# Seven-product V for the second pair of groups, moved from slots 11 to 17 into slots 72 to 84

## The chip, the cores and the metric

The kernel runs on one core of one Trainium2 chip. The metric is the time of one execution on the device, in microseconds (us); less is better. All data are fp32.

## The reference

One post-norm layer over a batch of two sequences of 512 tokens, width 512: grouped-query attention with 32 heads in 8 groups of 4, head size 128, and then a feed-forward block with four active low-rank experts. Cut to what matters here:

```python
q = hidden_states @ Wq + bq;  k = hidden_states @ Wk + bk;  v = hidden_states @ Wv + bv
q = _rope(q, pos);  k = _rope(k, pos)
scores = jnp.einsum('bgrsd,bgtd->bgrst', qg, k) / jnp.sqrt(D)
scores = jnp.where(causal, scores, finfo.min)
probs = softmax(scores)
ctx = jnp.einsum('bgrst,bgtd->bgrsd', probs, v)
x = layernorm(x + (ctx @ Wo + bo))
x = layernorm(x + ffn(x))
```

The change is about `v` (the projection of the hidden states by `Wv`) for one pair of groups and one batch, and about the addition of `bo`.

## The kernel before

**Units and slots.** A unit is one group of one batch: 16 units, in the order group 0 batch 0, group 0 batch 1, group 1 batch 0 and so on until the last two groups. The order of all work is written out by hand in slots. Slot T computes one block of scores (`score(T)`: 128 rows, which are 32 query positions of four heads), so a unit takes 16 slots (`UNIT`), and the widths within a unit go 32, 64, ... 512 columns because of the causal mask: score T has 32 x (T mod 16 + 1) columns, so that a slot can be found in the trace by the width. Four slots make a part p (a tile of 128 query positions). `slot(T)` emits, in this order: steps of the Q products, steps of the K or V products, the output products, score T, then `weigh` (context from weighted V, 12 slots after the part's first score); then the copies, maxima, exponentials and additions that belong to earlier slots; and last whatever was hung onto the slot with `put`. Each engine takes its instructions in the order in which they were emitted.

**What a score goes through.** TensorE writes score T to one of two PSUM buffers of tile `sc`. VectorE takes the masked maximum (L570), ScalarE the exponential (L577), and only then is the buffer free for score T + 2. VectorE inverts the sum (L581), ScalarE multiplies (L585), VectorE transposes in blocks of 32 (L593, L595). After a part's four slots the blocks are sent by SyncE's queue to memory (`db`, L603) and read back in the transposed arrangement (`pT`, L611), and `weigh` (L618) multiplies them with V.

**Products by seven.** Two neighbouring heads of Q, two groups of K or V, and two parts of the output projection are computed together as a 2 by 2 block product with seven instead of eight half products; the sums and differences of input blocks are formed first (`x_sums`, `w_sums`, `kv_sums`, `ctx_sums` on GpSimd, `wo_sums` on VectorE). Results are combined by copies on ScalarE (`q_copy`, `kv_out`) and additions on VectorE (`q_sum`, L490; `kv_out`, L546). A Q product that starts a new sum in the bank `qy` must wait until VectorE has added the bank's old content (L490).

**V.** V is made for pairs of groups: pair p is groups 2p and 2p + 1. Pair 0 is made plainly for both batches, by `v_tile`: for a tile of 128 tokens four products of 128 by 128 with 256 columns, in the PSUM tile `wx`, which the output products use only from slot 21 on, and then `v_out`, one copy on ScalarE (L357). Pairs 1 to 3 go by `kv_at`: in frames of 16 slots that begin at slot 8, 24, 40, ..., the four frames of a period hold K of batch 0, K of batch 1, V of batch 0 and V of batch 1 of the next pair, in seven steps (`KV_STEPS`: 0, 2, 4, 6, 8, 10 and 12 slots after the frame's start). The seven products of V need `kv_sums`, four operations on GpSimd, and end in four copies on ScalarE (L544) and three additions on VectorE (L546). One V is the exception: pair 1 of batch 0 (groups 2 and 3), which is made plainly in slots 11, 13, 15 and 17, so that the frame of slots 72 to 87 has no K or V products in it. Every V has its buffer out of three; V of pair 1 is first used by `weigh` in slot 76.

A plain tile and a step of seven, in the code's words (`product` for V is written out in `kv_products`):

```python
nc.tensor.matmul(psq["v", gg, t], lhsT=xT[:, c, ts(t, P)], rhs=wvs[gg][:, c, :], ...)      # x4 (c), 256 columns
nc.tensor.matmul(ps[:, ts(t, P)], lhsT=xt[:, c, ts(t, P)], rhs=w[:, c, :], ...)           # x2 (t) x2 (c), 128 columns
```

In the trace each fp32 product appears as two matmuls, each with its own weight load.

**Around slots 11 to 24.** These are the first slots with everything under way. VectorE also has here the rotations of Q and K (L378, L381, L385), the copies `lp_bc`, `arT`, `b_jar` and `bmT` of the feed-forward weights (slots 12 to 14; `arT` and `bmT` wait for small products `ta` and `tbm` that TensorE does in slots 13 and 14, after the slot's score and V tile), and the four sums of the first output weights (`wo_sums`, L647, slots 16 to 19). GpSimd has the second half of each rotation (L386), the weight sums of Q, the sums of contexts (L437 to L440), and eight additions of the output bias `bo` to the residual `x_sb`, one per token tile, in slots 12 to 19 (L906). The bias comes in a tile `bo_bc` of a pool that closes at slot 20, whose space goes to a pool (`late`) first written in slot 40 by `kv_sums`, on GpSimd too.

Of the kernel before, what the change touches and what calls it, by code (L numbers as in the profile page):

```python
# [12 lines left out]
ALU = mybir.AluOpType  # L13
# [4 lines left out]
G = 8  # L18
# [11 lines left out]
def postln_layer_kernel(  # L30
# [33 lines left out]
    nc = tc.nc  # L64
    B, S, HID = x.shape
    NT = B * S // P
    TPB = S // P
# [10 lines left out]
    UNIT = S // BLK  # L78
    VG = 2
# [30 lines left out]
    ps_wo = ctx.enter_context(tc.tile_pool(name="ps_wo", bufs=1, space=bass.MemoryType.PSUM))  # L110
# [3 lines left out]
    x_sb = const.tile([P, NT, HID], F32, name="x_sb")  # L114
# [34 lines left out]
    def load_k(g, queue=nc.sync):  # L149
        wk_g = wts.tile([P, KC, D], F32, tag="wk_g", name=f"wk_{g}")  # L150
        queue.dma_start(out=wk_g, in_=Wk[:, ts(g, D)].rearrange("(c p) n -> p c n", p=P))
        wqk["k", g] = wk_g
# [12 lines left out]
    def load_wv(gg):  # L165
        wv_g = wts.tile([P, KC, VN], F32, tag="wv_g", name=f"wv_{gg}", bufs=1)
        nc.sync.dma_start(out=wv_g, in_=Wv[:, ts(gg, VN)].rearrange("(c p) n -> p c n", p=P))
        wvs[gg] = wv_g
# [38 lines left out]
    bo_bc = setup.tile([P, HID], F32, name="bo_bc")  # L207
# [63 lines left out]
    def gather_experts(step):  # L271
        if step == 0:
            gather(ar_act[:EAR, :], lora_A.rearrange("e r n -> (e r) n"), idx["a"])
        elif step == 1:
            gather(ar_act[EAR : EAR + EA, :], router_W, idx["e"])
        else:
            a = step - 2
            gather(b_act[:, a, :], lora_B.rearrange("e (p j) r -> (e p) (j r)", j=BJ), idx["b"][:, a : a + 1])
# [65 lines left out]
    def v_mm(gg, t, c, pool, tag):  # L344

        if c == 0:
            psq["v", gg, t] = pool.tile([P, VN], F32, tag=tag, name="pv")
        nc.tensor.matmul(  # L348
            psq["v", gg, t], lhsT=xT[:, c, ts(t, P)], rhs=wvs[gg][:, c, :], start=(c == 0), stop=(c == KC - 1))

    def v_of(gg, b):
        if (gg, b) not in v_sb:
            v_sb[gg, b] = work.tile([P, TPB, VN], F32, tag="v", name=f"v_{gg}_{b}", bufs=3)
        return v_sb[gg, b]

    def v_out(gg, t):
        nc.scalar.copy(v_of(gg, t // TPB)[:, t % TPB, :], psq["v", gg, t])  # L357
# [77 lines left out]
    def strassen_sums(engine, a11, a12, a21, a22, s1, s2, s4):  # L435

        engine.tensor_tensor(s1, a21, a22, ALU.add)  # L437
        engine.tensor_tensor(s2, s1, a11, ALU.subtract)
        engine.tensor_tensor(s4, a12, s2, ALU.subtract)
        engine.tensor_tensor(a21, a11, a21, ALU.subtract)  # L440
# [59 lines left out]
    def kv_block(kind, p, h, c):  # L500
        if kind == "k":
            return wqk["k", VG * p + h][:, CH * c : CH * (c + 1), :]
        return wvs[p][:, CH * c : CH * (c + 1), ts(h, D)]

    def kv_sums(kind, p):
        w = kvs[kind, p] = late["pool"].tile([P, 3, CH, D], F32, tag="kvs", name=f"kvs_{kind}_{p}")
        strassen_sums(
            nc.gpsimd, *(kv_block(kind, p, h, c) for h in range(2) for c in range(2)), *(w[:, m] for m in range(3)))
# [376 lines left out]
    def put(slot, f):  # L885
        extra.setdefault(slot, []).append(f)
# [3 lines left out]
    def v_tile(gg, t, pool, tag):  # L890
        for c in range(KC):
            v_mm(gg, t, c, pool, tag)

    for k in range(2 + EA):
        put((-5, -4, -3, 7, 8, 9)[k], lambda k=k: gather_experts(k))
    for n, gg, t in [(n, 0, TPB + 1 + k) for k, n in enumerate((-4, 4, 6))] + [(2 * t + 11, 1, t) for t in range(TPB)]:
        put(n, lambda gg=gg, t=t: v_tile(gg, t, ps_wo, "wx"))
        put(n + 1, lambda gg=gg, t=t: v_out(gg, t))
    for k in range(2):
        put((5, 12)[k], lambda k=k: prior_weights(k + 1))  # L900
        put(13 + k, lambda k=k: lora_weights(k))
# [1 line left out]
    put(6, lambda: load_wv(1))  # L903
    put(17, lambda: load_wo(1))
    for t in range(NT):
        put(12 + t, lambda t=t: nc.gpsimd.tensor_tensor(x_sb[:, t, :], x_sb[:, t, :], bo_bc, ALU.add))  # L906

    def q_from(u, k):

# [15 lines left out]
    for p in range(1, G // VG):  # L925
        at = PERIOD * p
        put(13 if p == 1 else at - PERIOD + 9, lambda p=p: load_k(VG * p))
        put(37 if p == 1 else at - PERIOD + 13, lambda p=p: load_k(VG * p + 1))
        put(40 if p == 1 else at - 2 * UNIT + 3, lambda p=p: kv_sums("k", p))
        if p > 1:  # L930
            put(at - PERIOD + 37, lambda p=p: load_wv(p))
        put(at + (UNIT if p == 1 else 0) + 3, lambda p=p: kv_sums("v", p))

    def kv_at(T):

        frame, o = divmod(T - KV_FROM, UNIT)
        p, k = divmod(frame + B, VG * B)
        kind, b = "kv"[k // B], k % B
        if 0 < p < G // VG and (kind, p, b) != ("v", 1, 0):
            return (kind, p, b), o  # L940
        return None, None

# [6 lines left out]
    for n in range(NSETS - 2):  # L949
        at = {0: (-5, -4, -3, -2), NSETS - 4: (-16, -15, -15, -13), NSETS - 3: (-11, -9, -6, -5)}.get(n, (0, 1, 1, 3))  # L950
# [18 lines left out]
    def slot(T):  # L969
# [10 lines left out]
        if 0 < uk < PLAIN_K and l < KC:  # L980
            k_mm(uk, l)
        kv, o = kv_at(T)
        if kv and o in KV_STEPS:
            kv_products(*kv, KV_STEPS[o])
# [335 lines left out]
```

## Time and profile before

| | |
|---|---|
| time, median of 3 runs | 817.26 us (816.86 to 817.88) |
| time of the profiled execution | 816.9 us |
| its span, first to last instruction | 815.1 us |
| TensorE matmuls busy | 807.0 us (99%) |
| TensorE weight loads busy | 609.7 us (75%) |
| VectorE busy | 609.8 us (75%) |
| ScalarE busy | 384.9 us (47%) |
| GpSimd busy | 338.6 us (42%) |
| mean granted TensorE clock | 0.998 |

Starts and durations are in microseconds from the span's start. The profile names the engines PE (TensorE matmuls), PEld (TensorE's weight loads, which overlap the matmuls), DVE (VectorE), ACT (ScalarE), POOL (GpSimd) and SP (SyncE, which issues most transfers). The end of a matmul is modelled and overlaps the next one's start, so the price of a matmul is read from the distance of starts, not from its duration. A row of the timeline is a run of equal instructions: start, length, engine, line, operation, output<-inputs, shape and count; in brackets, how long the engine was idle before it and what ended that.

### The profile page before, as it was taken

To read this page: it belongs to the slowest core of one execution; us is meant where nothing else is said; L and a number is where in the kernel's file an instruction comes from. 1 tells how busy PE (TensorE), PEld (TensorE's weight loads), DVE (VectorE), ACT (ScalarE), POOL (GpSimd) and SP (SyncE) were. 2 spreads that over 40 slices of the span, in tenths; PEclk is the share of its full clock that TensorE was granted. 3 is DMA by queue.
4 is the path that set the end of the run, shared out by engine and by line. 5 is a ranking of instruction groups with operands and counts; after the bars stand their busy time and mean duration, and the time that the engine had idled before them with its cause. 6 is when DMAs were issued, how large, how long until landed. Compare 5 with 4: busy or idle time off the path is not lost.

```text
span 815.1 us, 11389 instructions
## 1 busy us (share of the span) xinstructions
PE 807.0 (99%) x3457; PEld 609.7 (75%) x3457; DVE 609.8 (75%) x1978; ACT 384.9 (47%) x1074; POOL 338.6 (42%) x392
## 2 busy tenths in 40 slices
PE   9999999999999999999999999999999999999996
PEld 7887777777777778777777778777777878656575
DVE  4778877687879886787867876787888689973455
ACT  2355454444545454545435454544545454663244
POOL 8666645421444345322443245343464333420033
PEclk9999999999999999999999999999999999999999
DMA  9025736355455637264544637365453726674211
GB/s 298 26 72 143 219 83 202 91 130 156 134 169 136 182 93 219 77 181 129 147 147 121 178 82 219 91 160 179 137 146 91 232 66 181 189 263 143 77 39 65
DMA packets 84415, 116.00 MB, mean 142 GB/s; under 512 B 6525, under 2 KB 64237, under 8 KB 82306
## 3 DMA queue, kind: packets, MB, share of 16 engines
q1 hardware_dynamic: 83154, 114.71, 49.0%
q8 instruction: 27, 0.44, 0.2%
q10 hardware_dynamic: 752, 0.42, 0.2%
q14 instruction: 34, 0.28, 0.1%
q0 software_dynamic: 448, 0.14, 0.1%
HBM read 71.21 MB, written 44.04 MB: 141 GB/s over the span
## 4 chain that ended last, share of the span: by engine, by line
PE 96%; POOL 1%; DVE 1%; ACT 1%; issue 0%; POOLq 0%
PE pc L618 17%; PE sc L562 15%; PE qx L450 14%; PE wx L450 12%; PE qy L450 10%; PE wy L450 9%; PE kx L450 4%; PE vx L528 4%; PE po L694 3%; PE py L788 3%; PE pv L348 3%; PE pp L365 1%; PE tp L285 1%; PE py L829 1%; POOL zt L191 0%; POOL act_er L220 0%
## 5 line engine op out<-in xcount | busy, mean ns | idle before, releaser
L577 ACT ACTIVATE p<-sc,nmax 128x288 f32<-128x288 f32 (+15 forms) x256 | 124.2, 485 | 197.7 <-DVE nmax L570 175.2
L570 DVE CUSTOM_DVE_ANT_0 sc<-sc,maskw 128x288 f32<-128x288 f32 (+15 forms) x256 | 114.2, 446 | 136.3 <-PE sc L562 134.7
L618 PE MATMUL pc<-pT,v 128*128 128x512 f32 x320 | 165.3, 599 | 0.0
L562 PE MATMUL sc<-kT,qT 128*128 128x160 f32 (+15 forms) x512 | 161.7, 398 | 0.3 <-ACT p L577 0.3
L386 POOL TENSOR_TENSOR qT<-q,t 128x512 f32<-128x512 f32 x64 | 88.0, 1376 | 176.1 <-DVE q L385 165.0
L585 ACT ACTIVATE p<-p,den 128x288 f32<-128x288 f32 (+15 forms) x256 | 133.2, 521 | 0.0
L562 PEld LDWEIGHTS sc<-kT,qT 128*128 128x128 f32 x512 | 96.1, 190 | 21.9 <-issue 8.1
L625 ACT ACTIVATE ctxT<-pc,bqkT 128x512 f32<-128x512 f32 x64 | 44.0, 688 | 114.8 <-PE pc L618 114.7
L437 POOL TENSOR_TENSOR cs<-ctxT 128x256 f32<-128x256 f32 x28 | 22.4, 801 | 158.5 <-PE wy L450 95.4
L593 DVE STREAM_TRANSPOSE zt<-p 128x128 f32<-128x128 f32 (+2 forms) x192 | 81.7, 426 | 0.0
L486 ACT COPY q<-qx 128x256 f32<-128x256 f32 x128 | 47.4, 370 | 51.4 <-PE qx L450 49.8
L618 PEld LDWEIGHTS pc<-pT,v 128*128 128x128 f32 x320 | 57.1, 190 | 18.7 <-issue 5.7
L450 PE MATMUL qx<-xs,wq 128*128 128x256 f32 x256 | 66.3, 381 | 0.0
L450 PEld LDWEIGHTS qx<-xs,wq 128*128 128x128 f32 x256 | 47.3, 190 | 23.2 <-issue 18.4
L595 DVE STREAM_TRANSPOSE zt<-p 128x32 f32<-128x32 f32 (+3 forms) x256 | 57.6, 225 | 0.0
L450 PE MATMUL wx<-wo,ctxT 128*128 128x256 f32 x224 | 57.5, 379 | 0.0
L378 DVE SCALAR_TENSOR_TENSOR t<-q,bqkT,rope_sb 64x512 f32<-64x512 f32 x64 | 52.3, 818 | 3.5 <-ACT q L486 1.7
L381 DVE SCALAR_TENSOR_TENSOR t<-q,bqkT,rope_sb 64x512 f32<-64x512 f32 x64 | 50.3, 786 | 1.5
L577 ACT ACTIVATION_READ_ACCUMULATOR p<-sc,nmax 128x1 f32 x256 | 49.8, 194 | 0.0
L385 DVE SCALAR_TENSOR_TENSOR q<-q,bqkT,rope_sb 128x512 f32<-128x512 f32 x64 | 48.1, 751 | 0.1
L450 PEld LDWEIGHTS wx<-wo,ctxT 128*128 128x128 f32 x224 | 42.5, 190 | 7.0 <-issue 1.4
L680 DVE TENSOR_TENSOR x_sb<-wx,x_sb 128x256 f32<-128x256 f32 x112 | 47.0, 420 | 0.0
(234 smaller groups left out, 1468.3 us busy)
## 6 DMA issues: line engine op xcount, KB each, us to landing
db<-zt SPq DMA_DIRECT2D x64, 256.0 KB, 4.3
pT<-db SPq DMA_DIRECT2D x16, 1024.0 KB, 4.8
db<-zt SPq DMA_DIRECT2D x64, 192.0 KB, 3.3
pT<-db SPq DMA_DIRECT2D x16, 768.0 KB, 4.4
wq<-in_L_attn_Wq_dram SPq DMA_DIRECT2D x20, 512.0 KB, 5.1
wo<-in_L_attn_Wo_dram SPq DMA_DIRECT2D x10, 1024.0 KB, 9.0
db<-zt SPq DMA_DIRECT2D x64, 128.0 KB, 2.4
pT<-db SPq DMA_DIRECT2D x16, 512.0 KB, 4.2
```

The source lines that it names most:

```text
L378: nc.vector.scalar_tensor_tensor(t2[lo, :], q[hi, :], b_ap[hi, :], rope_sb[hi, 1, :], ALU.add, ALU.mult)
L381: nc.vector.scalar_tensor_tensor(t2[hi, :], q[lo, :], b_ap[lo, :], rope_sb[lo, 1, :], ALU.add, ALU.mult)
L385: nc.vector.scalar_tensor_tensor(t1, q, b_ap, rope_sb[:, 0, :], ALU.add, ALU.mult)
L386: nc.gpsimd.tensor_tensor(dst, t1[:, :].rearrange("p (n s) -> p n s", s=BLK), t2[:, :].rearrange("p (n s) -> p n s", s=BLK), ALU.add)
L450: nc.tensor.matmul(ps, lhsT=wt[:, c, :], rhs=xt[:, c, :], start=start and c == 0, stop=c == CH - 1, skip_group_check=True)
L562: nc.tensor.matmul(sc[s][:, :w], lhsT=qT[u][:, i * QB + n].rearrange("p r s -> p (r s)"), rhs=kT[u][:].rearrange("p n s -> p (n s)")[:, :w ...
L570: nc.vector.tensor_tensor_reduce(sc[s][:, :w], sc[s][:, :w], maskw[:, S - w :], -SCALE, -MASKED, ALU.add, ALU.min, nmax[s])
L577: nc.scalar.activation(ptile[s][:, :w], sc[s][:, :w], AF.Exp, bias=nmax[s], scale=-1.0, accum_out=rden[s])
L585: nc.scalar.activation(ptile[s][:, :w], ptile[s][:, :w], AF.Copy, scale=rden[s])
L593: nc.vector.transpose(z[:, :, last - i : last, n, :].rearrange("p q j s -> p j q s"), ptile[s][:, : i * P])
L595: nc.vector.transpose(z[:, : n + 1, last, n, :], ptile[s][:, i * P : w])
L618: nc.tensor.matmul(psc[p], lhsT=v_sb[g // VG, b][:, j, ts(g % VG, D)], rhs=pT[p][:, :, ts(j, P)], start=(j == 0), stop=(j == i))
```

## The change

V of pair 1, batch 0, is no longer made by `v_tile` and `v_out` in slots 11 to 18. The exception in `kv_at` goes, so it is made by seven products in slots 72, 74, 76, 78, 80, 82 and 84, like all later ones, with copies and additions in slots 73 to 85. The weight sums for it (`kv_sums("v", 1)`) move from slot 83 to slot 67, because batch 0 now needs them too. Of the eight additions of the output bias, which were in slots 12 to 19, one each, the eight now stand in slots 11, 13, 15, 17, 19, 23, 26 and 28.

```diff
-    for n, gg, t in [(n, 0, TPB + 1 + k) for k, n in enumerate((-4, 4, 6))] + [(2 * t + 11, 1, t) for t in range(TPB)]:
-        put(n, lambda gg=gg, t=t: v_tile(gg, t, ps_wo, "wx"))
-        put(n + 1, lambda gg=gg, t=t: v_out(gg, t))
+    for k, n in enumerate((-4, 4, 6)):
+        put(n, lambda t=TPB + 1 + k: v_tile(0, t, ps_wo, "wx"))
+        put(n + 1, lambda t=TPB + 1 + k: v_out(0, t))
...
-        put(12 + t, lambda t=t: nc.gpsimd.tensor_tensor(x_sb[:, t, :], x_sb[:, t, :], bo_bc, ALU.add))
+        put((11, 13, 15, 17, 19, 23, 26, 28)[t], lambda t=t: nc.gpsimd.tensor_tensor(x_sb[:, t, :], x_sb[:, t, :], bo_bc, ALU.add))
...
-        put(at + (UNIT if p == 1 else 0) + 3, lambda p=p: kv_sums("v", p))
+        put(at + 3, lambda p=p: kv_sums("v", p))
...
-        if 0 < p < G // VG and (kind, p, b) != ("v", 1, 0):
+        if 0 < p < G // VG:
```

## The prediction

> **What bounds the kernel now.** I read the page first, then the waits of TensorE, then the timelines of TensorE and VectorE around slots 11 to 24, then the same for the frames after slot 72.
>
> ```profile
> span 815.1 us, 11389 instructions
> PE 807.0 (99%) x3457; PEld 609.7 (75%) x3457; DVE 609.8 (75%) x1978; ACT 384.9 (47%) x1074; POOL 338.6 (42%) x392
> PE sc L562 <- ACT p L577: 0.3, 1, 0.3
> ```
>
> TensorE is full, and its longest wait on a score is 0.3 us. A matmul taken out is time gained, provided that nothing else becomes the limit at that place. So two things must be found: the price of the plain V and of the seven products, and how much room the other engines leave in slots 11 to 24. First the price, from distances of starts (timeline of TensorE):
>
> ```profile
> 62.75 0.81 PE L562 MATMUL sc<-kT,qT 128*128 128x384 f32 x2
> 63.40 1.89 PE L348 MATMUL pv<-wv,xT 128*128 128x256 f32 x8
> 65.13 0.86 PE L562 MATMUL sc<-kT,qT 128*128 128x416 f32 x2
> ...
> 282.51 1.05 PE L528 MATMUL vx<-wv,xT 128*128 128x128 f32 x8
> 283.40 0.76 PE L562 MATMUL sc<-kT,qT 128*128 128x352 f32 x2
> ```
>
> A plain tile costs 65.13 - 63.40 = 1.73 us, a step of seven 283.40 - 282.51 = 0.89 us. Then the room (waits of VectorE from 63.3 to 91.95 us, and its timeline):
>
> ```profile
> DVE arT L296 <- PE ta L294: 2.4, 1, 2.4
> DVE sc L570 <- PE sc L562: 0.8, 1, 0.8
> DVE bmT L303 <- PE tbm L302: 0.6, 1, 0.6
> ```
>
> ```profile
> 71.26 0.31 DVE L296 COPY arT<-ta 128x144 f32<-128x144 f32 x1 [2.43 <-PE ta L294]
> 73.45 1.09 DVE L303 COPY bmT<-tbm 32x512 f32<-32x512 f32 x1 [0.58 <-PE tbm L302]
> 83.72 1.67 DVE L647 TENSOR_TENSOR wo<-wo 128x512 f32<-128x512 f32 x1
> 86.15 0.27 DVE L570 CUSTOM_DVE_ANT_0 sc<-sc,maskw 128x96 f32<-128x96 f32 x1 [0.76 <-PE sc L562]
> 91.62 0.42 DVE L490 TENSOR_TENSOR q<-qy,q 128x256 f32<-128x256 f32 x1
> ```
>
> This is the point of the case. From 63.3 us to the addition at 91.62 us VectorE is idle only 2.43 + 0.58 + 0.76 = 3.77 us, in 28.3. And at 91.95 us, when that addition ends, TensorE's next product into `qy` starts (92.09): it may not start earlier. In this stretch VectorE is nearly as full as TensorE.
>
> **What the change takes away.** 4 tiles x 1.73 = 6.92 us of TensorE in slots 11 to 17, and four copies of ScalarE (0.37 us each), which have no weight, since ScalarE is busy 13.5 of the 24 us there. No VectorE work goes. So if TensorE alone counted, it would stand 6.92 us earlier at slot 22. But the addition at 91.62 can come at most 3.77 us earlier, and TensorE waits for it. How much of the 3.77 is got: I move the rows up by what is gone.
>
> Slot 12: TensorE is 1.73 us earlier, at 63.75 us for the weight load of the first `weigh` (65.48 before), whose `pT` was issued at 61.45 and takes 3.2 us (the page's median for that size): 64.65, so TensorE waits some 0.9 us. It then comes to score 13 at about 66.1 + 0.95 - 0.4 = 66.7; the exponential of score 11, which frees the buffer and depends on VectorE's unchanged rows up to here, ends at 66.63. So score 13 starts near 66.7 (67.77 before), `ta` ends near 68.3. VectorE has finished what precedes `arT` at 68.83, so the 2.43 goes wholly. `tbm`: 68.3 + 0.94 (Q) + 0.81 (score 14) + 0.44 = 70.5, and 0.2 until VectorE starts; VectorE is there at 70.43: of the 0.58 some 0.2 to 0.6 stays (the end of that range if the first `pT` is later). The 0.76 goes, since score 18 is early. VectorE therefore gains 3.2 to 3.6 us, and TensorE with it; 3.4 is taken. What TensorE does in place of the other 3.5 us: it waits, at slot 20 most of all (score 20 needs the exponential of 18, whose maximum VectorE starts at 86.15 - 3.4 = 82.8, so it cannot start before 83.6, while TensorE would be there at about 82), and at slots 13, 16 and 22. After slot 22 VectorE has idle time in every slot (0.88 us at 97.52, then 0.3 to 1.4) and TensorE keeps its lead of 3.4.
>
> **What it adds.** Seven steps of 0.89 us are 6.21 us in slots 72 to 84. Whether they find room is read from frames of 16 slots, first score to first score:
>
> ```profile
> 235.85:277.18 41.33, 41.33 (x174) 31.26 (x173) 37.15 (x116) 20.99 (x61) 17.48 (x17) 1.00 0.60 163
> 277.18:323.83 46.65, 46.65 (x218) 36.49 (x216) 34.16 (x115) 22.21 (x65) 22.36 (x25) 1.00 0.51 150
> ```
>
> The columns after the length are TensorE, its weight loads, VectorE, ScalarE and GpSimd. The first frame is slots 72 to 87, without V or K except the 0.89 us with which the next begins: 40.44 without. The second is 88 to 103, with V of the other batch: 46.65 - 40.44 = 6.21. There is no slack to hide in: TensorE is busy all of 41.33, and no distance of starts there is stretched but one, by 0.08 us. So the whole 6.21 falls on the path. The three additions (0.42 us) and four copies fall into engines that are idle over 4 and 20 us of that frame; without that cover they would cost 2.7 us.
>
> At this price a rule of the Trainium skill speaks otherwise. "TensorE: Matmul & The Clock Gate", section "Back-to-back issue gap", says that weight load and matmul together set the distance in a stream, 81 ns at 128 columns and 131 at 512; a line through them gives 98 at 256. By it the seven would cost 56 x 81 = 4.5 us and the plain ones 32 x 98 = 3.1: the change would add 1.4 us of TensorE even if all of it were freed. The rows say 111 and 216 ns, so 6.2 against 6.9, a saving of 0.7. I take the rows.
>
> **What it moves.** `kv_sums` of V, four GpSimd operations (1.25 + 3 x 0.73 us), go from slot 83 to 67. Their tile is that of K's sums, which TensorE reads last in slot 68, so GpSimd waits, up to 4.7 us (the two later pairs: `POOL kvs_v L437 <- PE kx L450: 9.4, 2, 4.7`), and behind it stand a rotation, the context sums needed in slot 71 and weight sums. The frame from 370.30 to 416.81 us has that same sequence: its 46.51 us is 40.44 + 24 K products at 0.216 + 0.89 to 0.02. Taken at nothing; 1 us at most if a context sum were late. The bias additions (1.39 us each) leave slots 12 to 19 for 11 to 28. The first now stands ahead of the last rotation of unit 1, which ends near 70.4 instead of 69.2 and is needed by score 16, at 74. The last three are needed from slot 38. No transfer moves.
>
> They could help VectorE, though. The skill's "SBUF — State Buffer", section "Who interferes with whom", says that a VectorE instruction with two SBUF inputs and a GpSimd instruction that reads SBUF block each other. The row agrees: L647 took 1.67 us at 83.72 beside additions of bias, 0.68 at 81.34. By the rule VectorE's chain would shrink by up to 1.0 (this), 0.4 (L647 at 88.31, 1.10) and 0.35 (L381 at 87.19, 1.09): 1.7 us. But GpSimd does after the same rotation (81.57) still two additions and then the context sums, so the neighbours stay; I take none of it, and keep 1.7 for the range.
>
> **Sum.** -3.4 + 6.2 = +2.8 us on the profiled execution's 816.9 (815.1 span and 1.8 around it), which lies 0.4 below the median of the runs; the step is put on the median: 817.26 + 2.8 = 820.1.
>
> **Rivals.** (1) VectorE does not hold TensorE: then -6.92 + 6.21 = -0.7, 816.6. For it: TensorE does run up to 1.5 slots ahead of a maximum, and some lag can be carried. Against: the addition at 91.62 was already the last to arrive. It decides if VectorE's gain there passes 6.2; the idle time and the 1.7 make 5.5. This is the case that ends not slower. (2) VectorE's rows get shorter with the spread additions: a gain of 4 to 5.1, so +1.1 to +2.2, 818.4 to 819.5. (3) A transfer takes the place: `pT` of part 3 is issued at 93.41 and takes 4.8 (98.2), and its `weigh` starts at 99.53; it follows VectorE's transposes, and moves with VectorE, but with the 1 MB of `wo` issued at 81.39 it has only 1.1 us of room. If it, the first `pT` or the sums in slot 67 come late by 1 to 2 us, the result is 821.1 to 822.1.
>
> **How the numbers follow.** Forecast (820.1, own range 819.4 to 820.8): 0.66. Rival 1: 0.08. Rival 2: 0.11. Rival 3: 0.12. Something unforeseen that makes it faster: 0.03. The measurement can tell 0.2%, 1.63 us: below 815.6 faster, above 818.9 slower. Slower: 0.66 + 0.12 + 0.06 of rival 2 = 0.84; same 0.08 + 0.05 = 0.13; faster 0.03. The range of 8 in 10 takes in most of rivals 2 and 3: 818.5 to 821.8.
>
> **What would show it.** Right: slots 72 to 88 take about 6.2 us longer; score 24 starts about 3.4 us earlier than 99.04; in slots 13 to 22 TensorE waits some 3 us on ScalarE's exponentials (L577) and L490, and VectorE's idle time from 63 us on to the addition before slot 22 is near 0.5. Wrong: score 24 earlier by more than 5 us, VectorE's L647 below 1 us (rival 2), a wait of `pc` on `pT` in slot 24, or a frame of slots 72 to 87 longer than 47 us (rival 3).

## The result, and the profile after

The changed kernel takes 821.14 us (median of 6 runs, 820.83 to 822.16), the kernel before 817.28 us (6 runs): a ratio of 1.0049, with an interval of 1.0038 to 1.0059 (taken over all runs; the two medians alone give 1.0047). It is 3.9 us slower; 2.8 were forecast. The profiled execution took 820.84 us, of which 819.0 is its span. From the page, then TensorE's waits from 55 to 100 us (waiting instruction, what it waited for, total, times, longest):

```profile
span 819.0 us, 11441 instructions
PE 807.4 (99%) x3481; PEld 609.4 (74%) x3481; DVE 611.3 (75%) x1981; ACT 384.5 (47%) x1074; POOL 336.8 (41%) x392
PE sc L562 <- ACT p L577: 2.0, 2, 1.1
PE qy L450 <- DVE q L490: 1.0, 2, 0.5
```

TensorE's busy time hardly grew, and it still reads 99%. What is new are 3.0 us of waits in a stretch for which the same view of the kernel before is empty. The timeline of TensorE shows where:

```profile
62.55 0.81 PE L562 MATMUL sc<-kT,qT 128*128 128x384 f32 x2
64.42 0.97 PE L562 MATMUL sc<-kT,qT 128*128 128x416 f32 x2 [1.06 <-ACT p L577]
...
73.37 1.13 PE L450 MATMUL qy<-xT,wq 128*128 128x256 f32 x4 [0.54 <-DVE q L490]
...
84.02 0.54 PE L562 MATMUL sc<-kT,qT 128*128 128x160 f32 x2 [0.89 <-ACT p L577]
...
88.77 1.13 PE L450 MATMUL qy<-xT,ws 128*128 128x256 f32 x4 [0.41 <-DVE q L490]
...
95.73 0.65 PE L562 MATMUL sc<-kT,qT 128*128 128x288 f32 x2
```

Score 11 (384 columns) is followed at once by score 12 (416), the plain tile between them being gone, and score 12 must wait for the exponential of score 10 (352 columns), which ends at 64.3 on ScalarE:

```profile
63.73 0.55 ACT L577 ACTIVATE p<-sc,nmax 128x352 f32<-128x352 f32 x1 [1.08 <-DVE den L581]
```

Its maximum starts on VectorE at 63.10, right behind a rotation that takes 1.09 us, so that this wait, too, comes from VectorE.

Then come the two Q products that wait for VectorE's addition (slots 16 and 22), and score 20. Score 24 (288 columns) starts at 95.73; in the kernel before it started at 99.04:

```profile
99.04 0.65 PE L562 MATMUL sc<-kT,qT 128*128 128x288 f32 x2
```

The timeline of VectorE has almost no idle time left up to the addition that releases slot 22:

```profile
68.94 0.31 DVE L296 COPY arT<-ta 128x144 f32<-128x144 f32 x1 [0.32 <-PE ta L294]
69.16 1.13 DVE L297 COPY b_jar<-b_act 128x128 f32<-128x128 f32 x1
71.34 1.08 DVE L303 COPY bmT<-tbm 32x512 f32<-32x512 f32 x1
81.61 1.66 DVE L647 TENSOR_TENSOR wo<-wo 128x512 f32<-128x512 f32 x1
83.19 0.25 DVE L570 CUSTOM_DVE_ANT_0 sc<-sc,maskw 128x96 f32<-128x96 f32 x1
88.30 0.42 DVE L490 TENSOR_TENSOR q<-qy,q 128x256 f32<-128x256 f32 x1
```

Of 2.43, 0.58 and 0.76 us before, 0.32 is left. And the frame of slots 72 to 87, first score to first score (columns as before):

```profile
233.82:280.50 46.68, 46.68 (x221) 36.62 (x220) 36.74 (x118) 22.29 (x65) 12.94 (x13) 1.00 0.55 154
```

46.68 us, full, where it was 41.33. That is 5.35 more; the first of the seven steps stands just ahead of score 72 and adds its 0.89.

The first score starts at 43.97 to 44.18 us in some profiles of this study and at 44.80 to 45.01 in the others, whatever the kernel; so positions are compared from each profile's own first score. Counted so, against the first profile of before (a minus is earlier):

| start of score | 12 | 16 | 18 | 20 | 22 | 24 | 25 | 72 | 88 | 244 | 245 |
|---|---|---|---|---|---|---|---|---|---|---|---|
| changed kernel, us | -0.50 | -3.02 | -4.75 | -3.69 | -3.11 | -3.11 | -2.73 | -1.83 | +3.53 | +3.51 | +4.13 |

A lead of 4.75 us is built up as tiles disappear, and 1.6 of it is lost again in slots 20 to 22. Of the 6.92 us removed, 3.8 were therefore not had: 1.3 by score 13, 0.8 more by score 16, and these 1.6. A transfer takes 0.4 in slot 24. From slot 72 to 84 the seven steps take 0.89 us each (one of them before score 72): 6.26 in all. Another transfer takes 0.6 in slot 245. With the first score 0.2 us earlier, the sum is 3.9.

### The profile page after: what moved, and what is told of

Same layout as the page of the kernel before. It is cut to its first block, busy times and chain, and to the rows that moved or that the text cites. A ratio compares the mean times of both kernels' runs of the same rounds, so it can differ in the third digit from the quotient of the medians.

```text
span 819.0 us, 11441 instructions
## 1 busy us (share of the span) xinstructions
PE 807.4 (99%) x3481; PEld 609.4 (74%) x3481; DVE 611.3 (75%) x1981; ACT 384.5 (47%) x1074; POOL 336.8 (41%) x392
## 4 chain that ended last, share of the span: by engine, by line
PE 91%; DVE 4%; DMA 2%; POOL 1%; ACT 1%; issue 0%; SPq 0%; DVEq 0%; POOLq 0%
PE pc L618 16%; PE sc L562 13%; PE qx L450 13%; PE wx L450 11%; PE qy L450 9%; PE wy L450 8%; PE vx L528 5%; PE kx L450 4%; PE po L694 3%; PE py L788 3%; PE pv L348 2%; DMA db<-zt 1%; DMA pT<-db 1%; PE pp L365 1%; PE tp L285 1%; DVE sc L570 1%
## 5 line engine op out<-in xcount | busy, mean ns | idle before, releaser
L381 DVE SCALAR_TENSOR_TENSOR t<-q,bqkT,rope_sb 64x512 f32<-64x512 f32 x64 | 50.4, 788 | 1.5
```

The costliest lines, as they stand in the source:

```text
L381: nc.vector.scalar_tensor_tensor(t2[hi, :], q[lo, :], b_ap[lo, :], rope_sb[lo, 1, :], ALU.add, ALU.mult)
```

## The experiments

Theory H is the prediction's: in slots 13 to 22 VectorE and what hangs on it hold TensorE, so that most of the removed 6.9 us can't be had, while the added 6.2 counts in full. Times stand beside those of before on the same chip.

| kernel | time, us | before, us | ratio (interval) | score 24 | score 88 |
|---|---|---|---|---|---|
| changed kernel | 821.14 | 817.28 | 1.0049 (1.0038 to 1.0059) | -3.11 | +3.53 |
| V left out | 816.38 | 817.39 | 0.9992 (0.9985 to 0.9998) | -1.59 | -1.58 |
| V moved, additions not | 823.00 | 817.39 | 1.0072 (1.0058 to 1.0085) | -1.59 | +4.66 |
| V plain in slots 72 to 78 | 821.65 | 817.39 | 1.0049 (1.0036 to 1.0063) | -3.14 | +3.77 |
| changed, output sums on GpSimd | 820.85 | 817.39 | 1.0037 (1.0024 to 1.0049) | -4.66 | +1.59 |
| additions spread, V not moved | 816.97 | 817.59 | 0.9995 (0.9987 to 1.0004) | -0.24 | -0.23 |
| the same, output sums on GpSimd | 816.75 | 817.59 | 0.9996 (0.9987 to 1.0004) | -0.24 | -0.23 |
| changed, VectorE given more | 823.08 | 817.59 | 1.0068 (1.0051 to 1.0085) | -0.96 | +5.29 |
| changed, `wo` loaded later | 821.03 | 817.59 | 1.0050 (1.0033 to 1.0067) | -3.12 | +3.13 |
| changed, VectorE relieved twice | 819.47 | 817.19 | 1.0024 (1.0014 to 1.0034) | -5.14 | +1.12 |

**The removal alone.** V of pair 1, batch 0, is taken out of slots 11 to 17, and put nowhere.

```diff
-    ... + [(2 * t + 11, 1, t) for t in range(TPB)]:
...
-            psc[p], lhsT=v_sb[g // VG, b][:, j, ts(g % VG, D)], ...
+            psc[p], lhsT=v_sb[0 if (g // VG, b) == (1, 0) else g // VG, b][:, j, ts(g % VG, D)], ...
```

> The kernel before with V of pair 1, batch 0, left out altogether: its plain products in slots 11 to 17 are gone, nothing is put in slots 72 to 84, and weigh reads V of pair 0 in its place (so the output is another). The removal alone. Theory H (VectorE and the chains behind it hold TensorE in slots 13 to 22): TensorE comes to score 24 about 3.0 us earlier than before, not 6.9, and the time falls by 2.5 to 3.2 us, to about 814.5. Theory T (TensorE alone sets the pace, all removed products count): 6.9 us earlier at score 24, time about 810.4.

Theory T is out: 6.92 us of TensorE gone, and score 24 comes 1.59 us earlier. But H missed too, by half of its gain. The time fell by 1.0 us, and by 1.6 in the profile. In this kernel the bias additions are still in slots 12 to 19; the next run shows what that does.

**The move without the spread.**

```diff
-        put((11, 13, 15, 17, 19, 23, 26, 28)[t], lambda t=t: nc.gpsimd.tensor_tensor(x_sb[:, t, :], ...))
+        put(12 + t, lambda t=t: nc.gpsimd.tensor_tensor(x_sb[:, t, :], ...))
```

> The changed kernel with the eight bias additions back in slots 12 to 19; the move of V alone. H: the bias additions hide under GpSimd's idle time, so the same time as the changed kernel, +3.4 to +4.2 us over before; score 24 within 0.5 us of the changed kernel's. Theory B (the spreading of the additions costs part of the loss, by blocking VectorE or delaying GpSimd's sums): 1 us or more below the changed kernel, +2.9 us or less.

Both theories missed; the additions are not neutral, and spreading them is a help. With them in place the move costs 5.6 us instead of 3.9 (in the profiles, counted to score 245, 5.05 instead of 4.13), and score 24 is again at -1.59, as in the run before. GpSimd's timeline and VectorE's of this kernel:

```profile
68.94 6.19 POOL L906 TENSOR_TENSOR x_sb<-x_sb,bo_bc 128x512 f32<-128x512 f32 x5
81.98 5.09 POOL L906 TENSOR_TENSOR x_sb<-x_sb,bo_bc 128x512 f32<-128x512 f32 x3
```

```profile
73.94 1.75 DVE L378 SCALAR_TENSOR_TENSOR t<-q,bqkT,rope_sb 64x512 f32<-64x512 f32 x1
85.97 1.65 DVE L647 TENSOR_TENSOR wt<-wo,wt 128x512 f32<-128x512 f32 x1
```

And the changed kernel's rows to set beside them:

```profile
70.17 2.50 POOL L906 TENSOR_TENSOR x_sb<-x_sb,bo_bc 128x512 f32<-128x512 f32 x2
73.95 0.75 DVE L378 SCALAR_TENSOR_TENSOR t<-q,bqkT,rope_sb 64x512 f32<-64x512 f32 x1
85.00 1.10 DVE L647 TENSOR_TENSOR wt<-wo,wt 128x512 f32<-128x512 f32 x1
```

The rotation at 73.94 starts within GpSimd's run of five additions, which lasts until 75.13, and takes 1.75 us; the same rotation takes 0.75 in the changed kernel (at 73.95), where GpSimd has stopped at 72.67. In the kernel before it came at 76.07, after the run's end at 75.35, and took 0.75. The sum at 85.97 takes 1.65 beside the run of three, 1.10 in the changed kernel. The two make 1.55 us, and the leads of 3.11 and 1.59 differ by 1.52.

**V plain, but late.** Four plain tiles in slots 72, 74, 76 and 78, in the PSUM bank of K; additions spread.

```diff
+    for t in range(TPB):
+        put(72 + 2 * t, lambda t=t: v_tile(1, t, ps_k, "k"))
+        put(73 + 2 * t, lambda t=t: v_out(1, t))
```

> V of pair 1, batch 0, by plain products as before, but in slots 72, 74, 76 and 78; bias additions spread; kv_sums back in slot 83. The move without the seven products. H: gains 3.1 in slots 11 to 22, loses 4 x 1.73 = 6.9 in the frame of slots 72 to 87 (41.3 becomes 48.2 us), so +0.7 us against the changed kernel, +4.6 over before. Theory P (the loss comes from the seven products, whose short matmuls are dear): below the changed kernel, +1 to +3 over before.

The frame grows to 48.23 us, by 6.91. In the changed kernel the seven products cost 6.26: they are the cheaper way, by 0.65, and theory P is out. The measured times do not separate the two kernels: by score 245 the profiles differ by 0.2 us only, since this one has no wait for a transfer in slot 24 and a shorter one in slot 245.

**VectorE relieved.** The four `wo_sums` of the first output weights go to GpSimd, one slot earlier.

```diff
-        nc.vector.tensor_tensor(
+        engine = nc.gpsimd if n == 0 else nc.vector
+        engine.tensor_tensor(
             *((t1, b12, b11), (t2, b22, t1), (b12, b22, b12), (t4, b21, t2))[step], ALU.subtract)
...
-        at = {0: (-5, -4, -3, -2), ...
+        at = {0: (-6, -5, -4, -3), ...
```

> The changed kernel with the four sums of the first output weights (L647, 0.69 + 0.68 + 1.66 + 1.10 us of VectorE in slots 16 to 19) on GpSimd, in slots 15 to 18. H: VectorE has 4.1 us less to do between 73 and 86 us, so TensorE gains 2 to 3 us more in slots 13 to 24 (score 24 5 to 6 us earlier than before) until the transfer of part 3 or the waits of slots 13 to 16 hold it; time 818.0 to 819.2. Theory T or B or P: VectorE is not what holds, no more than 0.5 us better than the changed kernel, 820.6 or more.

Score 24 comes 4.66 us earlier, 1.55 more than in the changed kernel, and score 88 stands at +1.59 instead of +3.53 (0.4 of this is the wait of slot 24, which this profile does not have): VectorE was what held. The lead fell short of the 5 to 6 us, because the waits of slots 12 and 16 come before the sums and stayed. The time is still 820.85: the profiled run, 820.78, loses 1.6 us at slot 245, of which below, and its first score came 0.7 us later than in the profile of before. Whether the other runs near the median lost the same is not known; two of the six took 819.1 and 819.3.

**The same, with V not moved.** Two kernels: additions spread alone, and with the sums on GpSimd too.

> The kernel before with only the bias additions spread over slots 11 to 28; V stays plain in slots 11 to 17. In the run with V moved and the additions left in place, the additions blocked two of VectorE's rows (L378 1.75 us at 73.94, L647 1.65 us at 85.97). H (the additions matter only where VectorE has come forward into GpSimd's run of five): here TensorE is the limit until slot 17, so the time stays within 0.5 us of before. Theory B2 (the spread is worth some 1.5 us by itself): 815.9.

> The relieved kernel (sums of the first output weights on GpSimd, additions spread) with V back in slots 11 to 17, plain. H: relieving VectorE alone gives nothing where TensorE is full, 816.9 to 817.6, so that the move of V still loses 1.5 to 2.5 us even with VectorE relieved (its gain was 4.7 of 6.9 at score 24 and its price 6.2). Theory V (VectorE was the limit in the kernel before too): 1 us or more below before.

Neither can be told from the kernel before by its time, and both show the same 0.24 us from slot 22 on, the short wait for the addition L490 that the kernel before had there. Neither the spread nor the relief is worth more than that while the plain V is in slots 11 to 17. With VectorE relieved in both, moving V costs 1.59 + 0.23 = 1.8 us by score 88.

**VectorE given more.**

```diff
+    def sums_again():
+        nc.vector.tensor_tensor(wt[0][:, 0], wo_block(0, 0, 1), wo_block(0, 0, 0), ALU.subtract)
+
+    for s in (14, 15):
+        put(s, sums_again)
...
-        at = {0: (-5, -4, -3, -2), ...
+        at = {0: (-8, -4, -3, -2), ...
```

> The changed kernel with VectorE given more: the first of the four sums of output weights (L647, 0.69 us) comes in slot 13 and is done again in slots 14 and 15 (same result), 1.4 us of VectorE more before slot 22. H: VectorE is the limit there, so score 24 comes 1.4 us later than in the changed kernel (up to 2.9 if GpSimd's additions block the new operations), and the time rises as much: 822.5 to 824. If TensorE or a transfer were the limit: within 0.4 us of the changed kernel, 821.1.

Score 24 comes 2.15 us later than in the changed kernel, between the 1.4 and the 2.9: the sum that moved to slot 13 took 1.77 us beside GpSimd's additions, instead of 0.69. The time is 823.08. From slot 24 on this kernel recovers nothing of it; against the changed kernel the distance falls to 1.8 us, only because the changed kernel's wait for a transfer in slot 24 is absent here.

**The transfer of slot 24.**

```diff
-    put(17, lambda: load_wo(1))
+    put(25, lambda: load_wo(1))
```

> The changed kernel with the load of the second output weights (1 MB) moved from slot 17 to 25, behind the transfers of parts 3 and 4. H: TensorE's wait for pT in slot 24 (0.4 us in the changed kernel) goes, and nothing else does: 820.7, score 26 3.3 us earlier than before and not 2.9. If the transfers were what holds TensorE in slots 13 to 24: 1 us or more below the changed kernel.

TensorE's weight loads from 85 to 105 us, first in the changed kernel, then here:

```profile
PEld qy L450 <- DVE q L490: 1.2, 1, 1.2
PEld pc L618 <- DMA pT<-db: 0.6, 1, 0.6
```

```profile
PEld qy L450 <- DVE q L490: 1.2, 1, 1.2
PEld sc L562 <- ACT p L577: 0.2, 1, 0.2
```

The wait for `pT` is gone, score 25 stays at -3.12, and score 88 is 0.40 us better. The median, 821.03, is too coarse to show it. Nor does this one profile show that the load of `wo` was the cause: the kernel with V plain in slots 72 to 78 has the same slots 11 to 66 as the changed kernel, with `wo` in slot 17, and its profile has no such wait either. Counted from the first score, that `pT` landed at 52.5 and 52.6 us in the two profiles of the changed kernel, at 51.7 in the plain one, and at 51.2 here.

**VectorE relieved twice.** Sums on GpSimd, `wo` in slot 25, and the copies `arT`, `b_jar` and `bmT` on ScalarE.

```diff
-            nc.vector.tensor_copy(arT, ta)
-            nc.vector.tensor_copy(b_jar, b_act...)
-            nc.vector.tensor_copy(bmT[:EAR, :]..., tbm)
+            nc.scalar.copy(arT, ta)
+            nc.scalar.copy(b_jar, b_act...)
+            nc.scalar.copy(bmT[:EAR, :]..., tbm)
```

> The changed kernel with VectorE relieved twice: the four sums of the first output weights on GpSimd (slots 15 to 18), and the copies arT, b_jar and bmT of slots 13 and 14 (2.4 us of VectorE in the changed kernel) on ScalarE; the second output weights loaded in slot 25. H: the waits of TensorE at slots 16 and 20 go, that of score 12 for the exponential of score 10 (1.3 us) stays: score 24 comes 5.3 to 5.7 us earlier than before, the price of 6.2 later stays, so 0.5 to 0.9 us over before without what happens at the end, 818 to 819. If something other than VectorE holds TensorE there, score 24 stays at 4.7 us.

Its timeline of TensorE from 60 to 95 us has two waits left:

```profile
65.25 0.96 PE L562 MATMUL sc<-kT,qT 128*128 128x416 f32 x2 [1.06 <-ACT p L577]
83.81 1.12 PE L618 MATMUL pc<-pT,v 128*128 128x512 f32 x2 [0.41 <-DMA pT<-db]
```

The waits for L490 and for the exponential at score 20 are gone, and the lead is 5.14 us. It misses the 5.3 to 5.7 because a new wait stands in their place: part 2's `pT`, in slot 20, which the earlier TensorE now reaches before it has landed. What remains before it is the wait of score 12. Even this lead is smaller than the 6.26 us of the seven products, so that score 88 stands at +1.12. No version of the move that was tried beats the kernel before.

**The wait in slot 245.** Both kernels again, unaltered.

> The changed kernel again, unaltered, for the wait of TensorE on a transfer in slot 245 (0.6 us more than before in the first profile, though every issue up to it has the same distance). If it is scatter of landings: another value between 0 and 1.6. If it belongs to the change: 0.6 again.

> The kernel before again, unaltered, for the same wait in slot 245. If it is scatter: up to 0.6 us or more in some profile. If it belongs to the change: 0 to 0.1 again.

The changed kernel took 821.15 us, with score 24 at -3.13 and score 88 at +3.64; the kernel before took 817.79, within 0.07 us of its first profile up to score 244. The weight load of `weigh` in slot 245 waited 1.1 us for a `pT` in the changed kernel and 0.6 in the one before (1.0 and 0.3 in the first profiles). Over all profiles it is 0.3 to 0.6 us in the five where V is not in slots 72 to 84, and 0.6, 0.8, 0.8, 0.8, 1.0, 1.1, 1.1 and 2.0 in the eight where it is. So it scatters, and tends to be longer after the move. The four blocks (`db`) ahead of that `pT` are issued at the same distances in both kernels, but the third of them landed 4.1 and 4.0 us after its issue in the two profiles of the changed kernel, 3.3 in both of the kernel before, and `pT` is issued only after them. Why they land later stays open.

## Why the prediction was right, and where it was off

The direction and the mechanism held: TensorE at 99% was not free to give back what was removed. The size was forecast 1.0 us too small: 821.14 lies 0.3 us above the forecast's own range, within the wide one, and at the lower edge of what rival 3 would have given. The terms of the sum:

- **Removed, 6.92 us of TensorE.** Right in size, and, as predicted, more than half of it could not be had. The lead was sized at 3.4 us and measured 3.11, so that 3.8 was not had where 3.5 had been expected. That VectorE is what limits it is shown from both sides: taking work from VectorE gave 1.55 and 2.0 us more, adding work took 2.15 away.
- **Where TensorE waits.** Slots 16, 20 and 22 waited as said. The step for slots 12 and 13 failed: it had TensorE wait for the first `pT`, then at score 13 for the exponential of 11. It waited at score 12, for the exponential of 10, 1.06 us; by then the `pT` was there (issued at 61.17, landed 3.3 us later). The prediction passed over the score right behind the first removed tile. By it score 13 would have come 1.1 us earlier than before; it came 0.40 earlier. This wait stayed in every variant with V gone from slots 11 to 17; what would shorten it was not tried.
- **What stays of VectorE's idle time.** Some 0.2 to 0.6 was to stay at `bmT`; 0.32 stayed, at `arT`. The two belong together: `arT` waits for `ta`, which stands behind score 13 and ended at 68.9 us (69.1 counted from the first score of before), where 68.3 was expected. That the remainder was about as large as forecast is luck. VectorE's rows changed too: `b_jar` grew from 0.26 us to 1.13, and the L381 at 87.19 fell from 1.09 to 0.74. The growth comes with the removal and not with the spread: in all eight profiles in which V is gone from slots 11 to 17 and VectorE makes this copy, it takes 1.12 or 1.13 us, wherever the additions stand.
- **The spread additions, taken at nothing.** This step was wrong in its reason. The neighbours of VectorE's rows do not stay when VectorE moves by 2 to 3 us: with the additions left in place, the lead would have been 1.59. The move alone costs 5.6 us, and the spread gives 1.5 back in it by score 24 (1.1 by score 88, the wait of slot 24 being absent in that profile), though it gives only 0.24 us by itself. The sum for both together came out near by luck: in the kernel before, the rotation that the additions lengthen (at 76.07) came after them too, and took the same 0.75 us as in the changed kernel.
- **Added, 6.21 us.** Measured 6.26, with the frame at 46.68. The wait of `kv_sums` on GpSimd in slot 67 cost TensorE nothing. The estimate worked out from 81 and 131 ns was against the rows (111 and 216 ns), and the run with plain tiles settles it: plain 6.91, seven 6.26.
- **What was missing.** 0.4 us for `pT` in slot 24: rival 3's transfer, at a fifth to two fifths of its price, beside the forecast and not in place of it; it came in both profiles of the changed kernel, and its cause was not settled. 0.6 us at slot 245, unforeseen. The start gave 0.2 back. Forecast +2.8, less lead 0.3, these two 1.0, start -0.2: +3.9.

Rival 1 (no hold) fell with the run that left V out. Rival 2 (VectorE's rows get shorter) did not come: of its three rows only L381 got shorter, by 0.35 us, and `b_jar` took more than that away.

## What to carry to other kernels

Work that is taken from the fullest engine in one place and added in another is not a difference of two prices: ask for each place which engine is next, and how much idle time it has up to the next instruction that the full engine waits for. Idle time of the second engine before such an instruction (3.8 us here, of which 3.1 were had) bounds the gain as long as that engine's own work keeps its length, whatever was removed, while work that is added where the full engine has no gaps counts in full (6.26 us here). And when an engine moves forward in time, look anew at what runs beside it at that moment: here a rotation on VectorE took 0.75 or 1.75 us, depending on what GpSimd was doing.

## What was not expected of the hardware

A VectorE copy with one input, `b_jar` (128 by 128), took 0.26 us in the kernel before and 1.13 in the changed kernel. Its row of before, then GpSimd's rows beside it, before and after:

```profile
71.49 0.26 DVE L297 COPY b_jar<-b_act 128x128 f32<-128x128 f32 x1
69.16 6.19 POOL L906 TENSOR_TENSOR x_sb<-x_sb,bo_bc 128x512 f32<-128x512 f32 x5
68.94 1.26 POOL L386 TENSOR_TENSOR qT<-q,t 128x512 f32<-128x512 f32 x1
```

In both it ends about 0.1 us after a GpSimd operation does: at 71.74, where the second of the five additions ends at 71.66, and at 70.29, where the rotation ends at 70.21. The same holds in all twelve profiles in which VectorE makes the copy: it ends 0.08 to 0.09 us after a GpSimd operation. It takes 1.12 or 1.13 us where that operation had just begun, and 0.23 to 0.26 where it was nearly over. So not only operations with two SBUF inputs seem to be held until GpSimd's operation is over; this is inferred from the ends, and was not tried by itself. The Trainium skill's "SBUF — State Buffer", section "Who interferes with whom", does say that copies can enter a mode that takes both ports; the prediction used only its sentence on two inputs.
